# Layer 0's second product: one matmul of 96 output columns, or four column groups of 32 beside each other

## The chip, the cores and the metric

The kernel runs on one core of a Trainium2 chip. The metric is the device time of one launch in microseconds (us), lower is better. The core's engines run their own instruction queues in order: TensorE (PE, matmuls; its weight loads are listed as PEld), VectorE (DVE), ScalarE (ACT), GpSimd (POOL), and SyncE (SP), which here only issues DMAs. They wait for each other through semaphores.

## The reference

Four layers are applied to `x` of 32 images, 56x56 pixels, 96 channels, float32:

```python
# layer 0: an inverted bottleneck with weights mixed per image
rw = sigmoid(mean(x, (1, 2)) @ Wr + br)                         # 4 shares for each image
h  = relu(bn1(x @ einsum('be,ecm->bcm', rw, Wpw) + rw @ bpw))   # 96 -> 384 channels
h  = relu(bn2(conditional 3x3 depthwise filter of h))
h  = h @ einsum('be,emf->bmf', rw, Wpwl) + rw @ bpwl            # 384 -> 96: the second product
x  = bn3(h) + x
# layer 1: x + a 5x5 depthwise filter of x
# layer 2: relu, 3x3 depthwise filter, 1x1 product 96 -> 96, batch norm
# layer 3: a Swin block: layer norm, shifted-window attention (3 heads, windows of 7x7),
#          residual, layer norm, perceptron 96 -> 384 -> 96 with Gelu, residual
```

The change concerns the second product of layer 0: for each pixel of an image, 384 channels times a 384x96 matrix that was mixed for that image, plus a bias, plus the input.

## The kernel before

Four stages work on each image: the router (`stage_router`, line 848: pooling and mixed weights), the conditional layer 0 (`stage_conditional`, line 910), the filters of layers 1 and 2 (`stage_depthwise`, line 1018) and the Swin block (`stage_swin`, line 1170). `interleave` (line 1583) starts the four stages of four successive images together, so that in the steady part every image's router, conditional, depthwise and Swin work runs beside that of its neighbours.

The instructions are not issued as they are written. A `Recorder` notes each one with what it reads and writes (`call`, line 323) and a due time that comes from `PLAN` (line 162: for each stage a start and a length, in images). `order` (line 372) then plays the whole program through with a table of costs: whenever an engine is free, it takes the due-earliest work that is ready and whose buffers are free. `CROSSING` and `TO_TENSOR` are the delays that it assumes between engines, `CHANGE` is what it assumes for another tiling of TensorE, and `BESIDE` (line 170) is the number of matmuls that it assumes to run at the same time, by rows and columns of the tile. The resulting order of each engine's instructions is fixed in the program, and all of them are issued at line 578; this is why every line of the profile says L578 and groups are told apart by their tiles. Calls inside `chip.together()` stay beside each other.

Two kinds of instruction are made by the planner itself. Where PE has been idle in the plan for `SPARE_AFTER` ns, it puts in a filler, a 128x128 matmul of the identity into a free bank (`banks<-ident`). And two long DVE operations on SBUF may not stand next to each other: with `RUN = 1` the planner puts other work between them, or a one-element memset (`breath`).

Layer 0's conditional stage splits an image into two strips of 28 rows and, for each strip, the 384 channels into three blocks of 128. `expand` (line 916) multiplies by the first matrix in four pieces of 7 or 8 rows. ACT applies bias and relu into `h1`. The nine depthwise taps are one ACT operation and eight DVE operations `h<-h,mix,h` of 128x1568, which are DVE's main work. `relu` (line 976) finishes a block on ACT in two halves. When the three blocks `h2[0..2]` of a strip are done, `projections` (line 963) applies the second matrix: for each of the strip's four pieces of 7 rows (392 pixels) `project` (line 945) adds up three matmuls of 128 rows by 96 columns in one PSUM bank, and `add` (line 959) adds the bank, the bias and the input into `xT` on DVE. Projections are generated behind the taps of the next strip, so they are due among those. In the profile `project` is `banks<-h,wmix`, 128*96; `expand` is `banks<-xT,wmix`.

The Swin block's attention takes each image in eight rows of windows. `exponentials` (line 1223) makes the scores (`banks<-qT,kT`) and their exponentials on ACT; `kept` multiplies by the mask on POOL; `averaged` (line 1265) makes the softmax sums (`pair<-exps,ones`) and the weighted values (`pair<-exps,v`) in the two-bank tile `pair`, of which there is one, and ACT makes the reciprocal; `divided` (line 1298) divides on DVE in three operations and so frees `pair`. All other matmuls share six PSUM banks (`mm`, line 599). Each float matmul shows up in the trace as two passes with a weight load each.

Of the kernel before, what the change touches and what calls it, by code (L numbers as in the profile page):

```python
# [19 lines left out]
C = 96  # L20
# [3 lines left out]
P = 128  # L24
NB = 3
NROW = 8
RT = 7 * W
# [17 lines left out]
NSTRIP = H // STRIP  # L45
# [113 lines left out]
LANDING = 2200  # L159
IMAGE_LANDING = 10000  # L160

PLAN = {"router": (-0.309, 1.019), "conditional": (0.642, 1.103), "depthwise": (1.462, 1.483), "swin": (3.316, 0.933)}
CROSSING = 136

TO_TENSOR = {"vector": 981, "gpsimd": 1497, "scalar": 453, "sync": 1437}
SPARE_AFTER = 318
RUN = 1
CHANGE = 170
SAME = 0.0
BESIDE = {(32, 32): 16, (32, 64): 6, (64, 32): 6, (32, P): 3, (P, 32): 3, (P, P): 1}  # L170


def up(n):
# [3 lines left out]
def tiling(call):  # L177
    return tuple(up(n) for n in call[1][1].shape[:1] + (math.prod(call[1][1].shape[1:]),))


def tensor_time(calls):

    tiles = BESIDE[tiling(calls[0])]
    total = 30 if tiles > 1 else 0
# [107 lines left out]
class Recorder:  # L292
# [79 lines left out]
    def order(self):  # L372
# [50 lines left out]
        def done(w, now):  # L423
# [5 lines left out]
            for v in w.after:  # L429
                v.waits -= 1  # L430
                lag = 0 if v.engine == w.engine else TO_TENSOR[w.engine] if v.engine == "tensor" else CROSSING
                v.ready = max(v.ready, now + lag)
# [9 lines left out]
        def begin(w):  # L442
# [25 lines left out]
            if e == "tensor":  # L468
                heapq.heappush(events, (free[e] + SPARE_AFTER, count, None))
                count += 1  # L470
# [4 lines left out]
        while left:  # L475
            for e in self.ENGINES:
# [5 lines left out]
                while queues[e] and not unchanged:  # L482
                    item = heapq.heappop(queues[e])
                    w = self.work[item[1]]
                    if not available(w):
                        held.append(item)
                        continue
                    if e == "tensor" and SAME:
                        if first is None:
                            first = item  # L490
                        if item[0] > first[0] + SAME:
                            held.append(item)
# [37 lines left out]
                elif free[e] <= now:  # L530
                    seen[e] = changes[0]
                    if e == "tensor" and begun and self.spare and now >= free[e] + SPARE_AFTER and self.spare[2].free:
                        lhs, rhs, ring = self.spare
# [48 lines left out]
def kernel(  # L582
# [10 lines left out]
    def ring(name, shape, n):  # L593
        return Ring([const.tile(shape, F32, name=f"{name}{k}") for k in range(n)])
# [21 lines left out]
    x1s = ring("x1", [P, NQ, NBLK, W + 4], 2)  # L616
    x2s = ring("x2", [P, NQ, NBLK, W + 2], 2)
    filtereds = ring("filtered", [C + 1, H, W], 1)
    h1s = ring("h1", [P, STRIP + 2, W + 2], 2)
    if general:  # L620
        ss = ring("scores", [PK, NP, PK], 4)
# [55 lines left out]
    for k in range(NB):  # L677
        pt = mm.tiles[k]
# [16 lines left out]
    pt = mm.tiles[3]  # L695
# [31 lines left out]
    pt = mm.tiles[5]  # L727
# [27 lines left out]
    pt = mm.tiles[4]  # L755
# [87 lines left out]
    chip = Recorder(nc)  # L843
# [66 lines left out]
    def stage_conditional(b):  # L910

        xT, wmix, wmix2, mix, bias1, biasd, bias3 = mixed.pop(b)
        h1s_of = {}
        pieces = STRIP // 7
# [27 lines left out]
                at += n  # L942
                yield

        def project(n, h2):

            pt = chip.new(mm)
            with chip.together():
                for q in range(NB):
                    chip.tensor.matmul(  # L950
                        pt[:C, :RT],
                        wmix2[:, q * C : (q + 1) * C],
                        h2[q][:, n % pieces * RT : (n % pieces + 1) * RT].part(n % pieces // 2),
                        start=(q == 0),
                        stop=(q == NB - 1),
                    )
            return pt[:C, :RT]

        def add(n, y):
            rows = xT[:, 7 * n * W : 7 * (n + 1) * W].part(n)  # L960
            chip.vector.scalar_tensor_tensor(rows, y, bias3, rows, ALU.add, ALU.add)

        def projections(strip, h2):
            for n in range(pieces * strip, pieces * (strip + 1)):
                y = project(n, h2)
                yield
                add(n, y)
                yield

        blocks = [(strip, k) for strip in range(NSTRIP) for k in range(NB)]
        for _ in expand(*blocks[0]):
# [9 lines left out]
        h2 = {}  # L983
        for at, (strip, k) in enumerate(blocks):
            ahead = expand(*blocks[at + 1]) if at + 1 < len(blocks) else iter(())
            h1 = h1s_of[strip, k]
            h2[k] = chip.new(h2s).part(0, 1)
            acc = h2[k].rearrange("p (r w) -> p r w", w=W)
            for t in range(9):
                dy, dx = divmod(t, 3)  # L990
                tap = mix[:, k, t : t + 1]
                view = h1[:, dy : dy + STRIP, dx : dx + W]
                if t == 0:
                    chip.scalar.activation(acc, view, AF.Copy, scale=tap)
                else:
                    chip.vector.scalar_tensor_tensor(acc, view, tap, acc, ALU.mult, ALU.add)
                yield 2
                if t % 2 == 0:
                    next(ahead, None)
                    yield 1  # L1000
                if t == 1 and filtered_before:
                    relu(*filtered_before)
                if t > 1:
                    next(behind, None)
                    yield 1
            filtered_before = h2[k], k
            if k == NB - 1:
                for _ in behind:
                    yield 1
                behind = projections(strip, dict(h2))  # L1010
# [585 lines left out]
    def when(stage, b):  # L1596

        start, length = PLAN[stage]
        return b + start, length
# [5 lines left out]
    for step in range(B + 3):  # L1605
        stages = []
        b = step - 3
        if 0 <= b < B:
            stages.append((stage_swin(b, residuals.pop(b)), 148.5, when("swin", b)))
        b = step - 2  # L1610
        if 0 <= b < B:
            residuals[b] = []
            stages.append((stage_depthwise(b, residuals[b]), 49, when("depthwise", b)))
        b = step - 1
        if 0 <= b < B:
            stages.append((stage_conditional(b), 195, when("conditional", b)))
        if step < B:
            stages.append((stage_router(step), 12, when("router", step)))
        interleave(stages)
# [3 lines left out]
def build(nc, shapes, batch):  # L1623

    a = {k: nc.dram_tensor(f"in_{k}", s, F32, kind="ExternalInput").ap() for k, s in shapes.items()}
    layouts = {
        k: nc.dram_tensor(f"in_{k}", s, F32, kind="ExternalInput").ap()
        for k, s in (
            ("mask", (2, PK, NP, PK)), ("keep_last", (P, NP, WT)), ("keep_column", (P, WT)),
            ("k5", (P, NSLOT, 5, 2 * BIN)), ("k3", (P, NSLOT, 3, 2 * BIN)), ("centre", (P, 2 * BIN)),  # L1630
        )
    }

    out = nc.dram_tensor("out", (batch, NROW // 2, 2 * RT, C), F32, kind="ExternalOutput").ap()
    with tile.TileContext(nc) as tc, tc.tile_pool(name="flags", bufs=1) as flags:
        in_range = flags.tile([1, 1], mybir.dt.int32, name="in_range")
        tile_scores_in_range(tc, a, in_range)
        kernel(tc, a, layouts, out, False)

        with tc.If(nc.values_load(in_range[:1, :1]) < 1):  # L1640
            kernel(tc, a, layouts, out, True)
# [23 lines left out]
```

## Time and profile before

| | |
|---|---|
| median of 3 runs | 4646.62 us (4646.44 to 4652.35) |
| profiled execution, its own time | 4639.04 us |
| span of the profile | 4637.2 us |
| granted PE clock | 0.992 |
| PE busy | 4489.9 us, 97% |
| DVE busy | 4061.4 us, 88% |
| ACT busy | 3393.6 us, 73% |
| POOL busy | 2967.1 us, 64% |

The page is made from one profiled execution. A group's line gives engine, operation, what is written from what, the shape, the count, then the busy time, the mean length of one in ns, and the idle time before it with what ended it. `128*96` on a matmul means 128 rows by 96 columns of weights. A busy PE is not PE at its peak, because matmuls are pipelined: a pass of 392 columns is listed with some 494 ns, while the next one starts 329 ns after it. So starts are compared with starts here. Within the steady part one image takes 138.84 us, measured from one `pooled` to the next.

### The profile page before, as it was taken

The numbers are of one execution on the slowest core, as the hardware profiler recorded it, in microseconds if no ns is written. First come the engines' busy times: TensorE is split into PE (matmuls) and PEld (weight loads), VectorE is DVE, ScalarE is ACT, GpSimd is POOL, SyncE is SP. The second block draws the span as 40 slices with busy tenths as digits, with TensorE's granted clock in tenths as the row PEclk, the third lists the DMA queues.
The fourth block names the chain that finished last, engine by engine and source line by source line (L and its number), as shares of the span: only waits on it lengthen the run. The fifth ranks groups of instructions, "written<-read, shape, count | busy, mean of one in ns | idle before, by whom it ended". The sixth has DMA issues, their size and how long they took to land. (4 is left out here: it accounts for less than half of the span.)

```text
span 4637.2 us, 166483 instructions
## 1 busy us (share of the span) xinstructions
PE 4489.9 (97%) x71978; PEld 3168.6 (68%) x71978; DVE 4061.4 (88%) x5444; ACT 3393.6 (73%) x6625; POOL 2967.1 (64%) x1855
## 2 busy tenths in 40 slices
PE   5799999999999999999999999999999999999999
PEld 3566767676767676666676766666766676766677
DVE  6999999998999998999998999988999999999733
ACT  2467777777777777777787777777777787777666
POOL 3035767666767766767766767766767666767633
PEclk8999999999999999999999999999999999999999
DMA  2112111122111122211121211121211122211110
GB/s 54 34 39 45 41 43 32 39 48 45 44 41 30 38 47 45 45 40 30 38 47 45 46 40 30 38 45 45 46 41 30 38 45 45 46 41 31 28 36 22
DMA packets 556411, 185.36 MB, mean 40 GB/s; under 512 B 551679, under 2 KB 552340, under 8 KB 552596
## 3 DMA queue, kind: packets, MB, share of 16 engines
q1 hardware_dynamic: 555668, 174.61, 16.9%
q8 instruction: 569, 9.32, 0.9%
q14 instruction: 174, 1.43, 0.1%
HBM read 42.37 MB, written 38.54 MB: 17 GB/s over the span
## 5 line engine op out<-in xcount | busy, mean ns | idle before, releaser
L578 DVE SCALAR_TENSOR_TENSOR h<-h,mix,h 128x1568 f32<-128x1568 f32 x1536 | 2892.2, 1890 | 18.7 <-ACT h L578 13.0
L578 POOL TENSOR_TENSOR var<-var,mhalf 112x4 f32<-112x4 f32 (+1 forms) x512 | 1068.8, 2093 | 195.4 <-DVE var L578 182.8
L578 POOL TENSOR_TENSOR lnd<-res,var 112x384 f32<-112x384 f32 (+1 forms) x512 | 779.1, 1528 | 524.7 <-PE banks L578 503.0
L578 ACT ACTIVATE hid<-banks,c 128x448 f32<-128x448 f32 (+1 forms) x768 | 446.4, 589 | 346.5 <-PE banks L578 340.4
L578 PE MATMUL banks<-xT,wmix 96*128 96x392 f32 (+1 forms) x1536 | 644.2, 519 | 5.7 <-DVE wmix L578 4.5
L578 PE MATMUL banks<-hT,w 96*128 96x448 f32 (+1 forms) x1536 | 641.0, 507 | 3.7
L578 PE MATMUL banks<-x,band 32*32 32x280 f32 x24576 | 611.7, 408 | 14.8 <-issue 7.7
L578 PEld LDWEIGHTS banks<-w,hid 128*112 128x112 f32 x5376 | 563.9, 178 | 75.9 <-issue 46.2
L578 POOL TENSOR_TENSOR tb<-res,L_conv_b 112x384 f32<-112x384 f32 (+1 forms) x256 | 506.3, 1994 | 160.0 <-DMA out<-tb 139.1
L578 PE MATMUL banks<-w,hid 128*112 128x96 f32 x5376 | 576.2, 262 | 5.1 <-ACT hid L578 4.6
L578 PE MATMUL banks<-h,wmix 128*96 128x392 f32 x1536 | 548.4, 497 | 11.6 <-ACT h L578 11.6
L578 ACT ACTIVATE h<-banks,bias,s 128x392 f32<-128x392 f32 (+1 forms) x768 | 518.3, 690 | 39.0 <-PE banks L578 29.6
L578 PEld LDWEIGHTS banks<-x,band 32*32 32x32 f32 x24576 | 385.0, 103 | 226.7 <-issue 50.7
L578 POOL TENSOR_TENSOR exps<-exps,keep_column 49x147 f32<-49x147 f32 x224 | 396.2, 1769 | 204.1 <-ACT exps L578 194.0
L578 ACT ACTIVATE h<-h,biasd,s 128x784 f32<-128x784 f32 x384 | 389.3, 1038 | 114.0 <-DVE breath L578 83.6
L578 PEld LDWEIGHTS banks<-h,wmix 128*96 128x96 f32 x1536 | 246.5, 164 | 248.6 <-issue 207.2
L578 PEld LDWEIGHTS banks<-xT,wmix 96*128 96x128 f32 x1536 | 266.0, 192 | 134.0 <-issue 57.6
L578 DVE TENSOR_REDUCE var<-lnsq 112x4 f32<-112x388 f32 (+1 forms) x512 | 253.7, 496 | 113.3 <-ACT lnsq L578 59.8
L578 ACT ACTIVATE h<-h,mix 128x1568 f32<-128x1568 f32 x192 | 308.6, 1607 | 60.4 <-PE banks L578 46.4
L578 DVE SCALAR_TENSOR_TENSOR tb<-banks,res,tb 112x96 f32<-112x96 f32 x896 | 246.6, 308 | 109.2 <-PE banks L578 103.9
L578 PEld LDWEIGHTS banks<-hT,w 96*128 96x128 f32 x1536 | 252.5, 191 | 128.9 <-issue 69.1
L578 PEld LDWEIGHTS banks<-ident,lnd 112*96 112x96 f32 x1792 | 197.5, 126 | 157.0 <-issue 127.3
(135 smaller groups left out, 6653.0 us busy)
## 6 DMA issues: line engine op xcount, KB each, us to landing
x<-xT SPq DMA_DIRECT2D x1536, 35.0 KB
xT<-in_x SPq DMA_DIRECT2D x32, 1176.0 KB
filtered<-x SPq DMA_DIRECT2D x960, 35.0 KB
out<-tb SPq DMA_DIRECT2D x128, 168.0 KB
out<-tb SPq DMA_DIRECT2D x128, 126.0 KB
filtered<-x SPq DMA_DIRECT2D x576, 7.0 KB
band<-in_k SPq DMA_DIRECT2D x1, 960.0 KB
wpw<-in_L_conv_Wpw SPq DMA_DIRECT2D x1, 576.0 KB
```

What stands on the lines that cost most here:

```text
L578: getattr(getattr(self.nc, w.engine), method)(*args, **kw)
```

## The change

The second product is cut differently. A strip has four pieces of 7 rows, and the 96 output channels are three groups of 32. `round_of` takes piece `r` (0, 1 or 2) in its three channel groups on column groups 0 to 2 of the array, and on column group 3 the last piece's channel group `r`. All four write one bank, on 32 partitions each, and each is a sum over three matmuls of 128 rows by 32 columns. After three rounds all of the four pieces are done. The last piece's three parts lie on partitions 96 to 127 of three banks. ACT copies each into its place in a new SBUF tile, `last`, and one DVE `add` from it finishes that piece. `add` for the other three pieces is as it was. With the edit come other constants of the planner: due times of router, depthwise and Swin, assumed delays between engines, `SPARE_AFTER`, and four instead of three tiles of 128x32 beside each other.

```diff
-PLAN = {"router": (-0.309, 1.019), "conditional": (0.642, 1.103), "depthwise": (1.462, 1.483), "swin": (3.316, 0.933)}
-CROSSING = 136
+PLAN = {"router": (-0.16, 0.989), "conditional": (0.642, 1.103), "depthwise": (1.46, 1.448), "swin": (3.316, 1.102)}
+CROSSING = 412
 
-TO_TENSOR = {"vector": 981, "gpsimd": 1497, "scalar": 453, "sync": 1437}
-SPARE_AFTER = 318
+TO_TENSOR = {"vector": 926, "gpsimd": 865, "scalar": 129, "sync": 1437}
+SPARE_AFTER = 325
 RUN = 1
 CHANGE = 170
-SAME = 0.0
-BESIDE = {(32, 32): 16, (32, 64): 6, (64, 32): 6, (32, P): 3, (P, 32): 3, (P, P): 1}
+SAME = 0
+BESIDE = {(32, 32): 16, (32, 64): 6, (64, 32): 6, (32, P): 3, (P, 32): 4, (P, P): 1}
...
+    lasts = ring("last", [C, RT], 1)
...
-        def project(n, h2):
+        def round_of(r, h2):
 
             pt = chip.new(mm)
             with chip.together():
-                for q in range(NB):
-                    chip.tensor.matmul(
-                        pt[:C, :RT],
-                        wmix2[:, q * C : (q + 1) * C],
-                        h2[q][:, n % pieces * RT : (n % pieces + 1) * RT].part(n % pieces // 2),
-                        start=(q == 0),
-                        stop=(q == NB - 1),
-                    )
-            return pt[:C, :RT]
+                for k in range(NB):
+                    for at in range(pieces):
+                        n, g = (r, at) if at < pieces - 1 else (pieces - 1, r)
+                        chip.tensor.matmul(
+                            pt[32 * at : 32 * at + 32, :RT],
+                            wmix2[:, k * C + 32 * g : k * C + 32 * g + 32],
+                            h2[k][:, n * RT : (n + 1) * RT].part(n // 2),
+                            start=(k == 0),
+                            stop=(k == NB - 1),
+                        )
+            return pt
...
         def projections(strip, h2):
-            for n in range(pieces * strip, pieces * (strip + 1)):
-                y = project(n, h2)
+            last = chip.new(lasts)
+            for r in range(pieces - 1):
+                pt = round_of(r, h2)
                 yield
-                add(n, y)
+                chip.scalar.copy(last[32 * r : 32 * r + 32].part(r), pt[32 * (pieces - 1) :, :RT])
+                add(pieces * strip + r, pt[:C, :RT])
                 yield
-
-
+            for _ in range(1 if strip < NSTRIP - 1 else 0):
+                yield
+            add(pieces * strip + pieces - 1, last.part(*range(pieces - 1)))
+            yield
```

## The prediction

> **What bounds the kernel now.** First the page's totals, to see which engine is nearly full:
>
> ```profile
> PE 4489.9 (97%) x71978; PEld 3168.6 (68%) x71978; DVE 4061.4 (88%) x5444; ACT 3393.6 (73%) x6625; POOL 2967.1 (64%) x1855
> ```
>
> TensorE (PE) is, with VectorE (DVE) next. A busy PE is no proof of a bound, so the second view was the table by stretches over one image of the steady part, cut at each first matmul of the softmax sums (`pair<-exps,ones`, eight an image; the columns are length, then busy time and count of PE, PEld, DVE, ACT, POOL, granted clock, DMA share and GB/s):
>
> ```profile
> 2057.90:2137.60 79.70, 78.75 (x1123) 54.12 (x1120) 70.92 (x101) 60.12 (x115) 50.55 (x33) 1.00 0.22 50
> 2137.60:2146.00 8.40, 8.34 (x147) 5.81 (x146) 8.34 (x11) 7.45 (x18) 7.85 (x5) 1.00 0.17 35
> 2153.10:2160.40 7.30, 6.61 (x142) 5.27 (x141) 6.67 (x10) 6.76 (x15) 3.02 (x2) 1.00 0.01 3
> 2160.40:2167.20 6.80, 6.79 (x132) 4.60 (x132) 6.62 (x9) 5.14 (x10) 6.64 (x5) 1.00 0.01 2
> ```
>
> The long stretch (perceptron, band filters) is PE's: 78.75 of 79.70 us, DVE 70.92. In the short attention rows both are full. The starts of `pooled`, one an image, are 138.84 us apart on average over ten images; that is the period. Third, what PE does in it, in order of time (start, duration, count of passes; each float matmul is recorded as two passes):
>
> ```profile
> 2304.68 2.14 PE L578 MATMUL banks<-h,wmix 128*96 128x392 f32 x6
> 2306.75 0.55 PE L578 MATMUL pair<-exps,ones 49*32 49x196 f32 x12
> 2307.11 0.66 PE L578 MATMUL pair<-exps,v 49*32 49x49 f32 x48
> 2307.70 1.03 PE L578 MATMUL banks<-wo,oT 97*112 97x97 f32 x8
> 2315.36 2.14 PE L578 MATMUL banks<-h,wmix 128*96 128x392 f32 x6
> 2317.34 0.94 PE L578 MATMUL banks<-wv,slots 96*113 96x96 f32 x8
> ```
>
> One `project` takes 1.98 us from its start to the next group (2315.36 to 2317.34): 0.329 us a pass of 392 columns. Where the next group has another tiling it is 2.07. And `ones`: twelve passes of 196 columns need 12 x 0.164 = 1.97 us in a row, yet the next group starts after 0.36 us: three column groups on two row groups run beside each other, 5.5 of 6. Last, the waits and the fillers:
>
> ```profile
> PE pair L578 <- DVE oT L578: 24.8, 35, 2.4
> L578 PE MATMUL banks<-ident 128*128 128x128 f32 x1246 | 170.7, 289 | 33.7 <-ACT h L578 33.4
> ```
>
> PE hardly waits in the record because the planner fills planned idle time with `ident` matmuls (1246 passes are 623 fillers, 10 in each steady image). By start-to-start times an image's 138.84 us hold 3.0 us of fillers and at most 4.8 us of gaps; the rest is work.
>
> **What the skill says.** The Trainium skill, "TensorEngine Tiling (Array Packing)", Key Properties: tiles run independently, but "Changing tiling mode (not just tile) drains the TensorE". The trace agrees: going into a tiled group costs 0.09 us over a pass's own time, and coming out 0.085 to 0.105 us after the last tile has streamed. "TensorE: Matmul & The Clock Gate", Measured speedup vs the span model, has 2.38 for three column tiles; `ones` does better here. The same page, The mechanism, says that weight loads overlap running matmuls only when the row group differs. The trace speaks against that as the limit: in `ones` the second pass's loads start 0.026 us after the first passes on the same tiles. The tiling page's PSUM Bottleneck warns that emptying the banks does not get faster; that bears on part 4.
>
> **The change part by part**, for an image in the steady part.
>
> 1. Removed: 24 matmuls of 128x96 (8 pieces x 3), 48 passes charged 0.335 us each start to start: 16.08 us.
>
> 2. Added: 6 rounds of 12 matmuls, three steps of four tiles. A step has two passes. The moving data of four column groups over all 128 rows is as much as the 16 tiles of the band filter (`x,band`) read at a time; there the second pass starts 0.260 us after the first, for 280 columns of 0.235 us, and the third 0.236 later. So the first pass costs 0.026 more (`ones`: 0.190 against 0.164) and later ones nothing: 0.355 + 5 x 0.329 = 2.00 us, six rounds 12.0 us. No 128x32 tile is in the trace. From below the bound is 1.98 a round; from above, 2.38/3 of full overlap, 2.5 us a round. I take 2.00, by `ones`.
>
> 3. Changes of tiling: in the built programs' order a steady image has 43 before and 50 after (the rounds stand in four blocks: three together once, then three single). 7 x 0.092 = +0.64 us. Fillers go from 10 to 17. A filler takes at least 0.223 us (two passes, 0.112 each) and is charged 0.30 with its gaps: +1.56 us. From below nothing, if PE is idle there anyway; 2.1 from above. I take 1.56. Sum for PE: -16.08 + 12.0 + 0.64 + 1.56 = **-1.9 us** an image.
>
> 4. ScalarE (ACT) gets six copies of 32x392 from a bank; the nearest row, `qT<-banks` 96x392, is 0.484 us: +2.9 us on some 108 busy in 142, so idle time hides them. Without that cover they delay the bias-and-relu of `expand` and the Gelu queued behind, for which PE's banks wait. A bank now waits for a copy and an `add`, but an image takes 6 of them instead of 8. From below the ACT cost is nothing, from above 2.9.
>
> 5. DVE: eight `add`s as before, two of them from SBUF (0.634 us by `hid<-hid,hid`, against 0.617), and 15 `breath` memsets become 9: nothing. The last `add` waits for the third copy; behind it on DVE stand taps of the depthwise filter, so a late round would stop them. The first round needs the last relu's second half too, about 1 us later than the first piece needed before. No DMA is added; the order on SP and POOL changes only in how stages interleave.
>
> 6. Where the rounds stand. Before, the eight `project`s lie partly between attention rows as filling. After, one block of three rounds (6 us) stands in one row, the other three in the perceptron. I summed PE's work from `ones` to `ones`, calls times charged time: before 9.1, 7.2, 6.4, 6.5, 11.2, 7.4, 11.2, 81.8 us (sum 140.8; 0.977 brings the PE-bound part to the measurement); after 10.5, 5.7, 8.7, 11.7, 10.9, 10.0, 6.0, 76.1. No measured row is shorter than 6.80 us: the next row's sums need `pair` back from DVE, through exponential, sums, reciprocal and three DVE operations. Before, the two light rows took 7.32 and 6.80, 1.5 us over their scaled work. After, two rows of 5.55 and 5.8 (scaled) stretch to 6.8: 2.2 us. That is 0.7 to 0.9 us of new waits. Bounds: nothing, or as in the rival of the locked rows. I take 0.8.
>
> The period falls by 1.9 - 0.8 = 1.1 us. About 27 periods carry it: -30 us. At the start DVE is the bound (busy 137.4 of the 142 us from 142 to 284), and PE's gain and 14 more fillers vanish in idle time; at the end PE saves 3.4 us for each of two images and has ten more fillers: -5 us. The span goes from 4637.2 to 4602; with the 1.8 us around it the profiled execution, 4639.0, becomes 4604. The median of the runs is 7.6 us above that execution, so the forecast is **4612 us**, -0.75%.
>
> **The rivals.**
>
> *No new waits*: the gaps of before swallow the short rows. -1.9 x 27 - 5 = -56: 4591 us. For it: in the trace PE runs faster than planned around the fillers. Against: the 6.80 us floor is a chain through three engines.
>
> *The attention rows lock*: the slower case. If PE and DVE cannot make up in one row what they lost in another, because `pair` has one buffer and six banks bound PE's lead, each row takes the larger of the two. DVE's work in the rows (durations less 0.077 us of overlap) is 8.7, 7.3, 6.0, 6.5, 10.8, 8.2, 6.8, 70.1 before and 8.3, 7.9, 8.2, 9.1, 10.1, 9.1, 7.9, 64.0 after. The sum of the larger ones is 138.9 before, just what is measured, and 140.6 after; less 0.4 for the rounds, which these row sums charge at 2.15 us with their changes of tiling, and project, charged 0.66 a matmul there and 0.67 in part 1: +1.35 us, 27 x 1.35 = +36: 4683 us. It decides from the point where waits grow by more than 1.9 us an image. Against: rows of 5.55 us for PE beside rows of 10 leave room to catch up.
>
> *The change does not do what it says*: four column groups with all 128 rows do not fully overlap. At 2.5 us a round it costs 3 us an image: 1.9 us more than before, 4646 + 51 = 4698 us. My gain is gone at 2.18 us a round. `ones` speaks against it; that it uses only half the rows at a time speaks for it.
>
> *The gain is all lost*: fillers and gaps cost their 2.1 us and ACT some of its 2.9: 4645 us.
>
> **How the numbers follow.** Forecast 0.41 (its own range 4595 to 4632), no new waits 0.18, locked rows 0.22, no full overlap 0.11, all lost 0.08. Faster is the first two and a little of the last: 0.60; within 0.2%, about what a measurement of this kernel can tell from no change, 0.08; slower 0.32. The range from 4572 to 4690 cuts off the upper part of the slow rounds and some of the case without waits.
>
> **What would show it.** Right: a `banks<-h,wmix` group of 128*32 passes, about 2.0 us from a round's start to the next group (2.1 with the change of tiling), its four tiles some 7 ns apart; a period near 137.7 us; DVE's share up by half a point; copies of 0.48 us on ACT; rows with little work at 6.8 us. Wrong: rounds over 2.2 us; a period not under 138.5 with more `pair <- DVE oT` waits, or DVE waiting for `hid` or `last` in the attention rows; PE waiting for banks that a copy or an `add` still holds.

## The result and the profile after

The changed kernel is slower: 4670.53 us median against 4646.44, a ratio of 1.0051 with a 95% interval of 1.0035 to 1.0068. The forecast was 4612. Its profiled execution took 4675.21 us, with a span of 4673.3 us (before: 4637.2) and a granted PE clock of 0.990 (before: 0.992). The two profiled executions lie 36 us apart where the medians lie 24 apart, because that of before is 7 us under its median and this one 5 us over its own. So the size of the change is taken from the medians, and the profiles show where it arises. The totals of the page of the changed kernel:

```profile
PE 4471.0 (96%) x75462; PEld 3089.7 (66%) x75462; DVE 4110.1 (88%) x5284; ACT 3451.1 (74%) x6817; POOL 2677.8 (57%) x1855
```

PE is busy 19 us less, as a cheaper product should make it, and the span is 36 us longer all the same. DVE is the surprise: it has 160 instructions fewer and is busy 49 us longer. POOL has as many instructions as before and is busy 289 us less; the fifth point comes back to that.

First, did the new product do what it should? PE of the changed kernel in order of time (start, duration, engine, group, count of passes; an entry with 24 passes is one round, one with 72 three rounds):

```profile
2116.90 2.18 PE L578 MATMUL banks<-h,wmix 128*32 128x392 f32 x24
2119.01 1.02 PE L578 MATMUL banks<-hT,w 96*128 96x448 f32 x2
...
2186.71 6.13 PE L578 MATMUL banks<-h,wmix 128*32 128x392 f32 x72
2192.77 0.55 PE L578 MATMUL pair<-exps,ones 49*32 49x196 f32 x12
```

A round takes 2.11 us to the next group where that has another tiling (2116.90 to 2119.01), and the block of three 6.06 us, 2.02 each. Inside a block the second round starts 1.999 us after the first and the third 1.975 us after the second. The four tiles of a step start 7 ns apart; the next step starts 0.353 us after the first one of a block and 0.329 us after each later one. So four column groups over all 128 rows really run beside each other.

Second, the same cuts through one image as before, row of windows by row of windows (length, busy time and count of PE, PEld, DVE, ACT and POOL, granted clock, DMA share, GB/s):

```profile
2080.70:2155.20 74.50, 73.44 (x1057) 48.99 (x1057) 66.81 (x86) 54.39 (x102) 45.17 (x32) 1.00 0.21 48
2155.20:2166.10 10.90, 10.11 (x162) 7.09 (x163) 8.36 (x14) 10.90 (x27) 5.83 (x7) 1.00 0.21 42
2166.10:2172.10 6.00, 5.61 (x140) 4.44 (x141) 6.00 (x11) 4.89 (x13) 0.86 (x1) 1.00 0.08 16
...
2181.20:2192.80 11.60, 11.56 (x205) 6.27 (x206) 10.63 (x12) 7.42 (x15) 11.44 (x7) 1.00 0.01 4
...
2213.60:2220.70 7.10, 6.25 (x177) 4.38 (x178) 7.07 (x10) 6.39 (x14) 0.00 (x0) 1.00 0.26 58
```

The long stretch shrank from some 79.7 to 74.5 us, since the product has moved out of it. The seven other rows grew from 59.0 to 65.6 us together (medians before: 8.48, 7.05, 7.31, 6.80, 11.46, 7.18, 10.75; after: 10.88, 6.00, 9.17, 11.53, 11.28, 9.61, 7.09). A row of 6.00 us is there: my shortest row of 6.80 us is no floor.

Third, PE's time per image, start to start, over ten steady images. Each pass is charged until the next one starts, so the table adds up to the period:

| per image, us | before | after | |
|---|---|---|---|
| second product | 16.08 | 12.40 | -3.68 |
| fillers (`banks<-ident`, 128x128) | 3.01 | 6.85 | +3.84 |
| all other groups | 119.75 | 120.83 | +1.08 |
| period | 138.84 | 140.08 | +1.24 |

The line of the fillers in the changed kernel's groups (before: 1246 passes):

```profile
L578 PE MATMUL banks<-ident 128*128 128x128 f32 x1658 | 262.6, 293 | 47.5 <-ACT h L578 35.8
```

In the steady part 34 filler passes an image are charged 0.20 us each; before it was 20 at 0.15. What the product gave back stands at the fillers. Over the whole span: the 26 periods from the sixth `pooled` on take 28.8 us more, and both ends together 7.3 us more. The periods given below for the experiments are means of these 26: 138.8 us before, 139.9 after.

Fourth, the waits of PE and DVE in the changed kernel (total us, times, longest):

```profile
PE pair L578 <- DVE oT L578: 44.3, 64, 2.4
...
DVE var L578 <- POOL lnd L578: 112.8, 49, 6.9
...
DVE xT L578 <- ACT last L578: 58.6, 64, 5.8
```

PE's wait for `pair` went from 24.8 to 44.3 us. DVE's wait for POOL's normalised rows `lnd` more than doubled; this is its line before:

```profile
DVE var L578 <- POOL lnd L578: 51.7, 45, 5.7
```

The third line is new. The `add` of a piece starts only when ACT has copied the last piece's part out of the same bank, although both only read it: here the copy starts at 2188.96 and the add at 2189.47. First ACT, then DVE of the changed kernel, in order of time:

```profile
2188.96 0.48 ACT L578 COPY last<-banks 32x392 f32<-32x392 f32 x1 [0.43 <-PE banks L578]
```

```profile
2189.47 0.62 DVE L578 SCALAR_TENSOR_TENSOR xT<-banks,bias,xT 96x392 f32<-96x392 f32 x1 [0.79 <-ACT last L578]
```

The add is given to DVE with a wait for ACT. The Trainium skill, "PSUM — Partial Sum Buffer", section "PSUM bank collisions raise a hardware error", says that two engines may not touch the same bank and the same 32 partitions at once, reads included, but may touch different groups of 32. The copy reads partitions 96 to 127 and the add 0 to 95, so by that page this wait is more than is needed; the program keeps its readers apart by whole banks. No run here has them at the same time, so the page's statement isn't shown by one.

Fifth, DVE's groups. One operation on SBUF, the middle one of `divided`, has the same count and shape and became longer (count, busy us, mean ns, idle before). Before:

```profile
L578 DVE SCALAR_TENSOR_TENSOR hid<-hid,hid 96x392 f32<-96x392 f32 x256 | 162.3, 634 | 0.7
```

After:

```profile
L578 DVE SCALAR_TENSOR_TENSOR hid<-hid,hid 96x392 f32<-96x392 f32 x256 | 223.2, 872 | 0.7
```

These 61 us are 1.9 us an image, nearly all of DVE's 2.0 us more. By row the operation takes 796, 551, 829, 1178, 552, 2219, 552 and 588 ns; before it took 795, 553, 553, 657, 552, 553, 865 and 557. The row with 2219 shows why. DVE of the changed kernel in that row, and below it POOL in the same microseconds:

```profile
2206.14 0.56 DVE L578 TENSOR_TENSOR hid<-pair,hid 96x392 f32<-96x392 f32 x1 [0.35 <-ACT hid L578]
...
2208.75 2.23 DVE L578 SCALAR_TENSOR_TENSOR hid<-hid,hid 96x392 f32<-96x392 f32 x1
...
2212.67 0.55 DVE L578 TENSOR_TENSOR oT<-hid,pair 96x392 f32<-96x392 f32 x1
```

```profile
2206.48 2.67 POOL L578 TENSOR_TENSOR lnd<-res,var 112x384 f32<-112x384 f32 x1
2209.11 1.44 POOL L578 TENSOR_TENSOR exps<-exps,keep_last 128x588 f32<-128x588 f32 x1
```

The operation between two that read `pair` from PSUM reads both operands from SBUF. It starts while POOL's `lnd` is still running, and it lasts through the end of `lnd` and through all of POOL's mask, which starts 0.36 us after it. Both of these read SBUF too. Its neighbours with one operand in a bank keep 0.55 us. In the rows of 829 and 1178 ns it is POOL's `tb` and `lnd` that are under way when the operation starts, so the mask is not the only partner. In the order of before the same mask starts 0.33 us into the same operation, but POOL is idle until then, and the operation keeps its length. First DVE, then POOL of the kernel before, in order of time:

```profile
1626.08 0.55 DVE L578 SCALAR_TENSOR_TENSOR hid<-hid,hid 96x392 f32<-96x392 f32 x1
```

```profile
1626.41 1.52 POOL L578 TENSOR_TENSOR exps<-exps,keep_last 128x588 f32<-128x588 f32 x1 [4.12 <-ACT exps L578]
```

The Trainium skill, "SBUF — State Buffer", section "Who interferes with whom", says that a DVE instruction with two SBUF inputs contends with a GpSimd instruction that reads SBUF, that the order of issue decides which of the two blocks, and that a DVE instruction with at most one SBUF input does not contend. The trace agrees on who contends: 0.552 us in the undisturbed rows, 2.22 behind `lnd` and the mask. On the order it agrees for `lnd`, which was first; that the mask went ahead too, though it started later, is what this trace shows beyond the section.

POOL can be the one that waits. Its mask of the first seven rows, before and after:

```profile
L578 POOL TENSOR_TENSOR exps<-exps,keep_column 49x147 f32<-49x147 f32 x224 | 396.2, 1769 | 204.1 <-ACT exps L578 194.0 <-POOL h L578 0.7
```

```profile
L578 POOL TENSOR_TENSOR exps<-exps,keep_column 49x147 f32<-49x147 f32 x224 | 187.2, 836 | 493.1 <-ACT exps L578 418.5 <-ACT rw L578 50.7 <-PE pair L578 13.2
```

In the trace of before its long ones, 1.5 to 2.9 us, lie beside a DVE tap `h<-h,mix,h`. So before, more of the lost time fell on POOL, which is idle for 36% of the span; in the new order more of it falls on DVE.

### The profile page after: what moved, and what is told of

It is laid out like the page before. It is cut to its first block, busy times and chain, and to the rows that moved or that the text cites. A ratio compares the mean times of both kernels' runs of the same rounds, so it can differ in the third digit from the quotient of the medians.

```text
span 4673.3 us, 173505 instructions
## 1 busy us (share of the span) xinstructions
PE 4471.0 (96%) x75462; PEld 3089.7 (66%) x75462; DVE 4110.1 (88%) x5284; ACT 3451.1 (74%) x6817; POOL 2677.8 (57%) x1855
## 5 line engine op out<-in xcount | busy, mean ns | idle before, releaser
L578 POOL TENSOR_TENSOR var<-var,mhalf 112x4 f32<-112x4 f32 (+1 forms) x512 | 1000.2, 1963 | 222.4 <-DVE var L578 216.6
L578 POOL TENSOR_TENSOR lnd<-res,var 112x384 f32<-112x384 f32 (+1 forms) x512 | 844.0, 1655 | 56.4 <-PE banks L578 44.1
L578 PEld LDWEIGHTS banks<-x,band 32*32 32x32 f32 x24576 | 370.3, 103 | 245.0 <-issue 50.0
L578 POOL TENSOR_TENSOR exps<-exps,keep_column 49x147 f32<-49x147 f32 x224 | 187.2, 836 | 493.1 <-ACT exps L578 418.5
L578 PE MATMUL banks<-h,wmix 128*32 128x392 f32 x4608 | 408.4, 497 | 6.3 <-ACT h L578 6.3
L578 DVE SCALAR_TENSOR_TENSOR tb<-banks,res,tb 112x96 f32<-112x96 f32 x896 | 259.5, 309 | 93.1 <-PE banks L578 83.0
L578 PE MATMUL banks<-ident 128*128 128x128 f32 x1658 | 262.6, 293 | 47.5 <-ACT h L578 35.8
L578 PEld LDWEIGHTS banks<-h,wmix 128*32 128x32 f32 x4608 | 137.2, 110 | 256.9 <-issue 223.7
```

Source lines behind the costliest of these rows:

```text
L578: getattr(getattr(self.nc, w.engine), method)(*args, **kw)
```

## The experiments

The theories. **A**: the arithmetic of the product is right, and the new order of instructions loses the gain, because PE idles in it for other engines. **B**: fillers stand in PE's way and cost what they are charged. **C**: the copies and the bank's two readers hold up DVE and PE. **D**: DVE loses more time to POOL. Each ratio is against the kernel before as it ran beside that experiment; over the experiments its median lay between 4642.5 and 4651.4 us, so a difference between two experiments in microseconds is sure to some 10 us only. Where a kernel "keeps the order" of another, the plan is computed as for that one, and only the calls named are changed when the instructions are issued; everything else stands on each engine as it was.

**The product alone, with the planner's constants of before** (only the four tiles beside each other are taken over), and **the constants alone, with the product of before**:

```diff
-BESIDE = {(32, 32): 16, (32, 64): 6, (64, 32): 6, (32, P): 3, (P, 32): 3, (P, P): 1}
+BESIDE = {(32, 32): 16, (32, 64): 6, (64, 32): 6, (32, P): 3, (P, 32): 4, (P, P): 1}
-        def project(n, h2):
+        def round_of(r, h2):
...
```

> The changed product and evacuation with the planner's constants of before (and four tiles of 128x32). Theory 1, the new constants spoil the order and the product itself is worth its PE time: clearly under before, about 4610 us, a period near 137.5 us. Theory 2, PE's saved 3.7 us an image cannot be used because the attention rows hang on DVE and on the chain through pair, whatever the constants: 4640 to 4690 us, period 139 us or more.

```diff
-PLAN = {"router": (-0.309, 1.019), "conditional": (0.642, 1.103), "depthwise": (1.462, 1.483), "swin": (3.316, 0.933)}
-CROSSING = 136
+PLAN = {"router": (-0.16, 0.989), "conditional": (0.642, 1.103), "depthwise": (1.46, 1.448), "swin": (3.316, 1.102)}
+CROSSING = 412
...
```

> The product of before with the new planner's constants. Theory 1 (constants spoil): about 60 us over the changed kernel's place without product gain, 4700 to 4740 us. Theory 2 (the product's gain is not usable): within 25 us of before or of the changed kernel, 4640 to 4690 us.

Measured: 4773.15 us, ratio 1.029 (1.0268 to 1.0311), for the product alone; 4745.5 us, 1.0214 (1.0197 to 1.0231), for the constants alone. The product alone has a period of 143.1 us, again 34 filler passes an image, and a clock of 0.972, so that a part of its loss goes with the clock. With the constants alone the period alternates between about 151 and 133 us. Each half loses more than both together: what is compared are three orders, and each is worse than that of before.

**One assumed delay changed by 10 ns, nothing else:**

```diff
-CROSSING = 136
+CROSSING = 146
```

> The kernel before with one planner's constant moved by 10 ns (CROSSING 146 instead of 136). The plan comes out with another order: 14 or 15 fillers in a steady image instead of 10. Theory O, an order made anew without a search for constants is worse: 1 to 3% slower, 4690 to 4780 us, like the two half changes. If order hardly matters: within 0.4%, 4625 to 4665 us.

Measured: 4763.46 us, 1.0248 (1.0225 to 1.0272), period 143.7. Not one instruction of the kernel's work differs from before; only their order and the fillers do. So a plan made anew, for any reason, gave +2.1% to +2.9% in three cases and +0.5% in the changed kernel: before's order is the best of the five, and my sum silently assumed that the new order would be as good.

**Without fillers**, the changed kernel and the one before:

```diff
-    chip.spare = ident, ident, mm
```

> The changed kernel without the planner's filler matmuls (17 an image, charged 6.85 us of PE start to start). Theory F, fillers take PE time that real work would have used: the period falls by 2 us or more, under 4620 us. Theory I, fillers stand in time in which PE has nothing to do: within 0.4% of the changed kernel, 4655 to 4690 us, with PE waiting for pair and banks in their place.

> The kernel before without fillers (10 an image, charged 3.0 us). Theory F: about 1 to 2 us a period faster, 4590 to 4620 us. Theory I: within 0.3% of before, 4635 to 4660 us.

Measured: 4722.0 us, 1.0166 (1.0149 to 1.0183), and 4742.82 us, 1.0213 (1.0195 to 1.023). What the fillers were charged turned into waits. PE's wait for `pair` in the changed kernel without fillers, 44.3 us with them:

```profile
PE pair L578 <- DVE oT L578: 162.1, 145, 4.1
```

Two whole images of that kernel, in the table by stretches:

```profile
865.40:1005.20 139.80, 132.95 (x2309) 89.62 (x2307) 128.19 (x162) 107.36 (x214) 86.17 (x56) 1.00 0.18 41
1005.20:1150.60 145.40, 138.88 (x2309) 92.96 (x2308) 128.09 (x163) 107.87 (x214) 86.78 (x59) 0.95 0.18 39
```

At full clock an image takes 139.4 to 139.8 us without fillers (two images) and 140.1 on average with them. B falls for the changed kernel: 6.85 us of fillers stand in time in which PE waits anyway, and cost 0.7 us at most. What goes with taking them out is a lower clock: of sixteen images most are at 0.99 and some 140 us, and three at 0.95 and 145. The means over the span are 0.965 here, against 0.990 with fillers, and 0.954 against 0.992 in the kernel before. There no image without fillers ran at full clock (141 to 148 us at 0.94 to 0.98), so what its own fillers cost stays open.

**Less PE work in the order of before.** Of each strip's fourth `project` only the first of three matmuls is issued, 2.6 us an image less; and of all eight:

```diff
+calls = w.calls
+if w.engine == "tensor" and <weights are wmix2> and <piece 3 of the strip>:
+    calls = [(m, x, {**kw, "stop": True}) for m, x, kw in calls[:1]]
-for method, args, kw in w.calls:
+for method, args, kw in calls:
```

> The order of before is kept instruction for instruction, but the fourth project of each strip is one matmul instead of three (two of three terms of that piece are left out): PE has 2.6 us less to do an image, about the net of what the changed product saves, and nothing else is altered. Theory P, PE's time bounds the image: 2.6 x 27 = 70 us faster, about 4575 us. Theory R, in the order of before PE time is bound only in part of the image and the attention rows wait for DVE and pair: 10 to 40 us faster. If the saved time is worth nothing: within 9 us of before.

> The order of before kept; every project is one matmul instead of three (the terms of two of three channel blocks are left out): PE has 10.6 us less an image. Theory P: until DVE's 126 us bind, a period of 128 us, about 4360 us. Theory R: the gain stops where rows and DVE bind, 4540 to 4620 us.

Measured: 4578.6 us, 0.9861 (0.9844 to 0.9879), with 2.6 us less; 4647.97 us, 0.9998 (0.9979 to 1.0018), with 10.6 us less. The first shows that PE's time bounds the kernel before: its period is 136.6 us, 2.2 of the 2.6 us. The second shows that this ends. Two images of the kernel with 10.6 us less:

```profile
992.80:1128.00 135.20, 128.88 (x2200) 91.02 (x2199) 126.73 (x168) 105.88 (x208) 99.47 (x58) 1.00 0.19 42
1128.00:1269.50 141.50, 135.96 (x2200) 94.50 (x2200) 126.27 (x167) 106.47 (x208) 94.66 (x56) 0.94 0.18 40
```

The profiled execution is the slowest of twelve. At full clock an image takes 134.2 to 135.2 us, so 4 of the 10.6 us come back, and the rest is idle time of PE. Most images run at a clock of 0.94 and take 140 to 143 us, which undoes the 4 us. So the gain does not go on growing with the work taken away. It already stops between 2.6 and 4.0 us: a kernel with 4.0 us less, below, has the same period of 136.6 us as the one with 2.6.

**Less PE work in the order of after.** Of each round the first four of twelve matmuls, 7.9 us an image less:

```diff
+if w.engine == "tensor" and <weights are wmix2>:
+    calls = [(m, x, {**kw, "stop": True}) for m, x, kw in calls[:4]]
```

> The order of the changed kernel kept; each round is its first four matmuls instead of twelve (the terms of two channel blocks are left out): PE has 7.9 us less an image, 4 of them in one attention row, 4 in the perceptron. Theory P: 4670 - 7.9 x 27 = about 4460 us. Theory R, what PE saves there comes back as waits for DVE and pair: 4600 to 4670 us.

Measured: 4612.11 us, 0.9913 (0.9879 to 0.9946). At full clock its images take 136.8 us, 3.2 of 7.9 us less than the changed kernel's; some at a clock of 0.92 take 144. The row of three rounds lost 2.6 of its 4 us, and rows behind it took part of that back. PE's wait for `pair`:

```profile
PE pair L581 <- DVE oT L581: 112.8, 92, 3.4
```

I had hoped that this run would tell the two orders apart, and it does not: 40% come back here, and 40% of 10.6 us in the order of before. PE's time is worth something in both. What tells them apart is the idle time to begin with: 6.85 us of fillers an image that can go without a loss at full clock, against 3.01 us of fillers before. That is A, and it asks what PE waits for.

**The mask on POOL taken out**, in the order of after and in that of before:

```diff
+if w.engine == "gpsimd" and calls[0][0] == "tensor_tensor" and <output is exps>:
+    calls = []
```

> The order of the changed kernel kept, the mask's multiplication on POOL is left out. In the changed kernel the DVE operation hid<-hid,hid takes 0.872 us on average against 0.634 before, 2.22 us in one row of each image in which it overlaps POOL's mask and lnd operations. Theory S, this collision stands in the chain that bounds the rows: the operation falls to about 0.65 us, the period by 1.2 us or more, under 4640 us. Theory N, the rows do not hang on it: within 0.3% of the changed kernel, 4656 to 4684 us.

> The kernel before in its own order with the mask's multiplication on POOL left out; the control for the same edit in the changed kernel, which gained 43 us. If the mask's collision with hid<-hid,hid belongs to the new order alone: within 0.3% of before, 4630 to 4660 us. If the mask costs every order: 30 to 50 us faster, about 4600 us.

Measured: 4627.45 us, 0.9959 (0.9945 to 0.9974), after, 43 us less than the changed kernel; 4650.62 us, 1.0007 (0.9999 to 1.0014), before. The same work on POOL costs 43 us in one order and nothing in the other. The DVE operation in the order of after without the mask:

```profile
L581 DVE SCALAR_TENSOR_TENSOR hid<-hid,hid 96x392 f32<-96x392 f32 x256 | 173.0, 676 | 0.7
```

It goes from 872 to 676 ns; what is left over 552 is beside `lnd` and `tb`. But POOL itself has less to do there too, so this run doesn't say how much is the collision. Nor does the run in the order of before: there the operation takes 643 ns without the mask and 634 with it, so the mask was not what lengthened it, and the collision stayed.

**One operand of that DVE operation read from the bank**, so that it has one input in SBUF and POOL keeps all its work:

```diff
+if w.engine == "vector" and calls[0][0] == "scalar_tensor_tensor" and calls[0][1][2] == 2.0:
+    calls = [(m, (x[0], self.pair[:C, :, : NP * WT], *x[2:]), kw)]
```

> The order of the changed kernel and its mask kept; the middle operation of the division reads the bank pair instead of hid (it computes something else), so that only one of its inputs lies in SBUF. Theory S, DVE's two-input operations on SBUF and POOL's exclude each other: its mean falls from 0.872 to about 0.56 us, and the period by 1.2 us or more as without the mask, about 4625 us. Theory L, the mask's own time in the chain from exponential to sums was the cost: the mean falls, the time stays at 4655 to 4680 us.

Measured: 4646.25 us, 1.0000 (0.999 to 1.0009), 24 us less than the changed kernel. The operation in that kernel's groups:

```profile
L582 DVE SCALAR_TENSOR_TENSOR hid<-pair,hid 96x392 f32<-96x392 f32 x256 | 141.3, 552 | 0.7
```

The kernel then computes something else, but issues as many instructions. The operation takes 552 ns in all rows, 320 less, 82 us in all; 24 us of it come back, and the period falls to 139.1 us. PE's wait for `pair` falls back to that of before (24.8 us, and 44.3 in the changed kernel):

```profile
PE pair L582 <- DVE oT L582: 24.2, 59, 2.4
```

Over the same ten images as in the table, the fillers are charged 5.96 us instead of 6.85 and all other groups 120.62 instead of 120.83. So D is shown: taking the collision away gives back 24 us, as much as the change cost by the medians. That the sizes match is no proof that nothing else is lost, for this edit may help a kernel beyond what the change took. It was not made in the order of before, where the operation could give back 82 ns x 256 = 21 us of DVE time at most; at the share that came back here, 24 of 82, that would be some 6 us (an estimate).

What D does not explain is the gain that is missing. Without the collision the changed kernel is level with before, and the forecast lay 34 us lower. In its steady part the product is still 3.68 us cheaper than before, and the fillers take 2.95 us of that and all other groups 0.87.

**The rounds in the order of before.** The plan is that of before; at each place of a `project` of pieces 0 to 2 a round is issued, with the copy ahead of its `add`; the fourth `project` falls away. A round whose inputs are not all there yet is held until the last half of `relu` has been issued:

```diff
+if n == 3:
+    return
+if not all(u in self.given for k in range(NB) for u in h2[k].buffer.relus):
+    self.late.append(w)
+    return
+for k in range(NB):
+    for at in range(4):
+        m, g = (n, at) if at < 3 else (3, n)
+        self.nc.tensor.matmul(pt[32 * at : 32 * at + 32, :RT], <wmix2 of k, g>, <h2[k] of piece m>, ...)
...
+self.nc.scalar.copy(self.last[32 * n : 32 * n + 32], <bank>[96:, :RT])
+self.nc.vector.scalar_tensor_tensor(*args, **kw)
```

> The plan of before is kept: every instruction of every engine stands where it stood, but when the program is given out, the first three projects of a strip become the three rounds, the fourth becomes nothing, a copy to last stands ahead of each of the first three adds, and the fourth add reads last. PE saves 3.7 us an image and has nine more changes of tiling (0.8 us). Theory O, the rounds are worth their time and the new order lost it: 2.5 to 3 us a period, 4560 to 4590 us. Theory E, the copies, the fuller dependence on h2 or the banks spoil it: 4630 us or more.

Measured: 4703.54 us, 1.0123 (1.0098 to 1.0148): worse than either kernel. The first `pooled`s come 40 us later up to the sixth, and the 26 periods after that take 139.8 us each. DVE's largest wait in it:

```profile
DVE xT L600 <- ACT last L597: 202.0, 124, 13.9
```

That is C, in this order. Six kernels take it apart.

**Without the copies** (`last` stays zero), in this order and in the changed kernel's own:

```diff
-self.nc.scalar.copy(self.last[32 * n : 32 * n + 32], <bank>[96:, :RT])
```

> As the rounds in the order of before, with the three copies left out: last is zero, the fourth add reads it (the last piece's product is left out of the result, while PE computes it). Theory W: 4560 to 4590 us, what the rounds alone are worth. Theory B: 4680 us or more, the rounds do not pay in this order even without copies.

```diff
+if w.copy:
+    continue
```

> The changed kernel in its own order with the three copies left out (last is zero, so the last piece's product is missing from the result). Theory W, the adds that wait for ACT's copy hold DVE back here as in the order of before, where the copies cost 66 us: 1.5 to 2 us a period, 4610 to 4635 us. Theory N, in this order, which was planned with the copies, they are hidden: 4656 to 4684 us.

Measured: 4637.3 us, 0.9975 (0.9964 to 0.9986), in the order of before; 4667.5 us, 1.0031 (1.0022 to 1.004), in the order of after. Copies cost some 67 us in an order that was not planned for them. In the changed kernel they cost 3 us by the medians and 9 by the ratios, with intervals that overlap (1.0022 to 1.004 without them, 1.0035 to 1.0068 with them). DVE's wait in the changed kernel without copies:

```profile
DVE xT L581 <- issue: 28.5, 58, 2.3
```

58.6 us of waiting for `last` became 28.5 us of other idle time, and the end hardly moved. So C is a small part of the slower result at most. The kernel in the order of before has a period of 137.7 us, the very one I forecast, 1.1 us below that of before. Its sixth `pooled` comes 28.7 us late, though, and most of the gain goes there.

**The fourth `project` taken away and no more**, in the order of before with 96-column projects; and with the **first `project` reading piece 3**, so that it waits for the last half of `relu` like a round does:

```diff
+if n == 3:
+    return
```

> The order of before; the first three projects of a strip as before, the fourth left out, its add reads a zero tile. PE saves 4.0 us an image with no change of tiling and no new wait. It is the rounds without copies (4637 us) less their tiling and less their dependence on the last relu. If PE's time keeps its worth of before (64 us for 2.6 us an image): 4545 to 4565 us. If it saturates: about 4575 us.

```diff
+m = n if n else 3
...
-    h2[k].found()[:, n * RT : (n + 1) * RT],
+    h2[k].found()[:, m * RT : (m + 1) * RT],
```

> As the fourth project removed, but the first project multiplies the last piece's rows instead of its own (a wrong result), so that it waits for the second half of the last relu as a round does, in the place in which a round is given out. If this wait is what the rounds lost: near 4637 us, most of it in the first four images. If the nine further changes of tiling are: 4550 to 4580 us.

Measured: 4584.04 us, 0.9845 (0.9824 to 0.9867), and 4601.33 us, 0.9873 (0.9852 to 0.9893). With each kernel's median taken against that of before beside it, the steps in the order of before are: 67 us gained by 4.0 us less product an image; 17 lost by the later input, mostly before the sixth `pooled` (11 us in the traces; the period is 136.6 and 136.7 us); 38 lost by 32-column rounds in place of projects (period 136.7 to 137.7; nine more changes of tiling an image); 68 lost by the copies. The late start is not the later input alone: with the fourth `project` away and nothing else the sixth `pooled` is already 16.5 us late. Up to it the granted clock is 0.91, against 0.95 before; whether that is the cause is not shown.

**The `add` issued ahead of the copy**, in that order and in the changed kernel's own:

```diff
-self.nc.scalar.copy(self.last[...], <bank>[96:, :RT])
 self.nc.vector.scalar_tensor_tensor(*args, **kw)
+self.nc.scalar.copy(self.last[...], <bank>[96:, :RT])
```

> As the rounds in the order of before, but the copy to last is given out behind its add instead of ahead of it. There, DVE's adds waited 202 us in all for the copy of the same bank: in the program the add carries a wait for ACT, no longer one for PE alone. Theory W, this wait on DVE ate the rounds' gain: DVE's waits for last fall under 60 us and the time to 4560 to 4600 us. Theory B, it is the rounds themselves or the six copies on ACT: 4680 to 4720 us as with the copy ahead.

> The changed kernel in its own order, the copy held back until its add is given out. DVE waits 58.6 us for last there, 1.8 us an image. Theory W: 1 to 1.8 us a period less, 4620 to 4645 us. Theory B, or if the rows bind anyway: within 0.3% of the changed kernel, 4656 to 4684 us.

Measured: 4823.45 us, 1.037 (1.0337 to 1.0403), and 4696.08 us, 1.0094 (1.0069 to 1.0119). Both are worse, so the repair that C suggests is none. Now ACT waits, and its queue behind it; ACT's line in the waits of the first of the two, whose clock was 0.957:

```profile
ACT last L600 <- DVE xT L597: 95.3, 74, 6.0
```

So in both orders it was the better choice that DVE's `add` waits for ACT's copy, although DVE is the busier engine. That the whole 120 us of the first come from ACT's wait is argued, not shown; its clock is lower too.

None of the versions that compute all of the result beat the kernel before.

## Why the prediction was wrong

Two steps failed: step 3 priced the fillers at 1.56 us an image, and step 5 put DVE at nothing.

**What bounds the kernel: right, for a small step.** 2.6 us less on PE took 2.2 to 2.4 us off an image of the kernel before; 4.0 us less took no more off its period.

**Steps 1 and 2, the product: right.** 16.08 us went, 12.40 came, with the changes of tiling behind the rounds in it; a round is 1.975 to 2.02 us where I had 2.00. The rival of rounds that don't overlap is dead.

**Step 3, the fillers: here the sum failed.** Forecast -16.08 + 12.0 + 0.64 + 1.56 + 0.8 = -1.08 us; measured -16.08 + 12.40 + 3.84 + 1.08 = +1.24. Of the 2.3 us between them the fillers are 2.28. The other terms (0.64 for tiling and 0.8 for waits against 1.08 measured, and 0.4 in the product) make up for each other. I took fillers for work with a price of 0.223 us. They mark idle time of PE in the plan: seven more of them an image said that the planner itself saw more of it, and the time at them more than doubled, where removing them gave back 0.7 us at most. I had that number, from 10 to 17, before the result, and read it as a cost instead of as a warning that PE would wait more. Of the 3.84 us, 0.9 go away with the collision of step 5; what PE waits for in the rest stays open.

**Step 4, ACT's copies: right for this kernel, for a reason that I hadn't checked.** They cost 3 to 9 us of 4670 here. The cover belongs to the order: without it they cost some 67 us. That the `add` would wait for the copy of its own bank I had only as "a bank waits for both".

**Step 5, DVE at nothing: wrong.** The adds and memsets cost nothing, as said. What moved was the neighbourhood: `hid<-hid,hid` waited longer for POOL's `lnd`, `tb` and mask, and DVE got 2.0 us an image longer. It frees `pair` later, and PE waited 20 us more for `pair`. Taking the collision out returned 24 us of the 58 between forecast and measurement, and those 20 us of waiting. The row of this operation stood in the page before with 634 ns against 552 for its neighbours of the same size, and that excess was the sign that it has a price which depends on POOL.

**Step 6, where the rounds stand: wrong.** The two light rows took 6.00 and 7.09 us instead of 6.8 twice, so there is no floor at 6.80; and rows with much work also grew over PE's own (10.88 over 10.3, 9.17 over 8.5, 11.28 over 10.65 by the prediction's scaled sums). My 0.8 us was in the wrong place.

**The ends: wrong.** -5 us forecast, +7.3 measured; the start is longer by more than the end is shorter.

**The rivals.** The locked rows forecast a period 1.35 us longer and 4683 us; 1.24 and 4670.53 were measured. The size and sign are right, the mechanism only in part. PE does wait for DVE by way of `pair`. But each row is not the larger of PE's and DVE's work: a row with 7.9 us of DVE work took 6.00, and rows 10.88 where the larger was 10.3. That DVE lost time to POOL was in none of my cases.

**Left out of the cases altogether**: that a new plan could be worse than the old by itself. Three other plans made anew came out 2.1, 2.5 and 2.9% slower than before.

**What stays open.** Where the 34 us between the forecast and the level of before went. By the trace most of them stand at the fillers, but no run shows what PE waits for there. DVE's 61 us more of waiting for POOL's `lnd` in the order of after are one candidate, which was not tried alone; they are not the 24 us, since 112.5 us of this wait remain where the collision is out and the time is level with before. Open too is whether an order exists in which the rounds gain what the period of 137.7 us promises, without the 29 us at the start; no full version was found.

## What to carry to other kernels

When a planner orders the instructions, price the new order, not the edit: count its own marks of idle time (fillers here) and read more of them as PE waiting more for others. Test what an engine's time is worth by shortening its work in a fixed order, and by a small step: 2.6 us gave 2.2 here, while 10.6 us gave 4 in the images at full clock and nothing in the median. And look for operations whose mean is above that of equals with one operand in PSUM, because they are the ones whose price depends on what POOL is doing.

## What the hardware showed that I had not expected

- Four 128x32 column groups ran fully beside each other: 24 passes of 392 columns in 1.975 us, tiles 7 ns apart. A strip's fourth piece thus takes no further time on PE.
- A 96x392 DVE operation with both operands in SBUF took 0.552 to 2.22 us depending on what POOL did; with one operand in PSUM it stayed at 0.552. A mask that started inside it cost it nothing where POOL had been idle, and its whole length where POOL came from `lnd` without a pause.
- Where much of PE's work was left out its clock was lower, by whole images: with two thirds of the product left out images took 134 to 135 us at 1.00 or 140 to 143 at about 0.94; without fillers 140 at 0.99 or 145 at 0.95. With 2.6 or 4.0 us less an image it stayed at 1.00 over the 26 periods.
